# A fused attention and deformable-convolution block: the front's steps in halves, the convolution's PSUM emptied by ScalarE

## The chip, the cores and the metric

The kernel runs on one core of a Trainium2 chip. The metric is device time in microseconds (us) of one execution, lower is better. The engines are TensorE (PE; its weight loads are listed apart as PEld), VectorE (DVE), ScalarE (ACT), GpSimd (POOL) and the queue of SyncE (SP), which only issues transfers. Each engine works through its own list of instructions in the order in which the kernel wrote it.

## The reference

Two layers, each with a residual, on x of shape 8 x 256 x 64 x 64 in float32. `_gn` is a group normalisation over 32 groups.

```
x = x + L0(_gn(x))     # L0: q, k, v by a 1x1 convolution; 4 heads; softmax over the 3x3
                       # neighbours of each pixel; a second set of 3x3 weights generated from
                       # q, k, v; alpha * generated + beta * softmax weights v; projection
x = x + L1(_gn(x))     # L1: modulated deformable 3x3 convolution: a 3x3 convolution gives
                       # offsets and masks; each of 9 taps samples 4 corners of the image at
                       # its offset, mixes them bilinearly, times the mask; then 256x9 -> 256
```

## The kernel before, in words

One image is held in SBUF (`image`), in 8 chunks of 8 rows (512 pixels). Its work falls in two parts. The *front* is layer 0 and the preparation of layer 1: `attention(b)` runs the normalisation and the attention chunk by chunk, and `prepare(b)` writes the second normalisation's result to a table in DRAM (`to_table`), computes the offsets (`offsets`) and turns them into indices and weights (`positions`). The *back* is the deformable convolution. A chunk has 9 taps; a tap of a chunk is a *slot*, so an image has 72 slots, and a slot has 4 blocks of 128 pixels.

For each block of the back POOL gathers 128 table entries of 4 KB (`gather`), ACT scales the first corner (`scale`), DVE adds the three others (`sum_corners`, three instructions per block), PE turns the sum (`transposes`, two per block into `pt`), ACT copies `pt` to SBUF (`vt`), and PE multiplies by the tap's weights (`product`, four matmuls into the PSUM tile `po`, which gathers all 9 taps of a chunk in two banks, one for each half `m` of the output channels). After the ninth tap `finished` adds x1, the result of layer 0, to `po` and stores it. x1 was written to DRAM by `second_stats` (`kept`) and is read back into `r` in the middle of the chunk.

The loop at the end of `preact_kernel` (L891 to L910) writes out the order by hand for PE, ACT, DVE and POOL. It merges the back of image b with the front of image b+1. Slot n is: `transposes(n)`; `ahead(4n)`, which scales blocks 8 and 9 ahead, sums blocks 6 and 7 ahead (six DVE instructions) and gathers blocks 18 and 19 ahead; `product(n-1)`; then the front's steps that are due; then `ahead(4n+2)`. After every ninth tap both `ahead`s stand before `product`, and `finished` after it. The front is a generator that yields 73 times per image; the pace lets about one step run in each slot. A chunk of attention is seven steps, named below by what they hold: *q* (L579 to L583: `spread_weights` of the chunk before, then q), *k*, *products*, *logits*, *v0*, *v1*, *weights* (the last with `project(1)`, the add into x1, the statistics and `keys(0)`). The first image's front runs alone, before any slot; the last image's back runs alone, after all fronts.

Lines that matter below: `psum_a` (L190) hands out four PSUM buffers in turn for all of the front. `spread_weights` (L487) fills all four with `wk` matmuls (L492), and DVE empties them by multiplying with a mask (L500). `q` (L288) then asks for the same buffers (L293). `finished` (L856) has DVE read `po` (L859). `po` has a single buffer, so the next chunk's first tap (L848) waits until it has been read.

Of the kernel before, what the change touches and what calls it, by code (L numbers as in the profile page):

```python
# [17 lines left out]
P = 128  # L18
C = 256
# [33 lines left out]
STEPS = 2 + 7 * NC + 6 + NC + 1  # L53
STEPS_AHEAD = 6
# [3 lines left out]
def preact_kernel(ctx: ExitStack, tc: tile.TileContext, a: dict, out: bass.AP):  # L58
# [126 lines left out]
    wp = ctx.enter_context(tc.tile_pool(name="wp", bufs=NC + 3))  # L185
# [93 lines left out]
    class Attention:  # L279
# [70 lines left out]
        def products(self):  # L350


            self.qk = qk = p1.tile([P, NB, NT, 2, NK], F32, tag="qk", name=f"qk_{self.u}")
            for jj in range(NB // 2):
                both = [psum_a(f"qk_{self.u}_{jj}_{h}") for h in range(2)]
                for ct in range(NT):
                    for j in range(2):
                        for t in range(2):
                            o = 2 * (2 * jj + j) + t
                            for h in range(2):  # L360
                                r = slice(64 * h, 64 * h + 64)
                                n = (2 * j + ct) * NK
                                nc.tensor.matmul(  # L363
                                    both[h][64 * t : 64 * t + 64, n : n + NK],
                                    self.qt[r, ct, o * T * T : (o + 1) * T * T],
                                    kt[r, ct, :, T * o : T * o + KT],
                                    start=True,
                                    stop=True,
                                )
                for h in range(2):  # L370
                    nc.vector.tensor_mul(  # L371
                        qk[:, 2 * jj : 2 * jj + 2, :, h, :],
                        both[h][:, : 4 * NK].rearrange("p (j c k) -> p j c k", j=2, c=NT),
                        near_k.unsqueeze(1).unsqueeze(1).to_broadcast([P, 2, NT, NK]),
                    )

        def logits(self):
# [3 lines left out]
            by = p1.tile([P, G * KT, 3], F32, tag="by", name=f"by_{self.u}")  # L381
# [94 lines left out]
        def weights(self):  # L476
            ps = psum_a(f"w_{self.u}")
            for j in range(NB):
                nc.tensor.transpose(
                    ps[:, j * P : (j + 1) * P],  # L480
                    wts2[self.c % 2][:, j].rearrange("p h k -> p (h k)"),
                    ident,
                )
            self.wsb = p1.tile([P, N], F32, tag="wsb", name=f"wsb_{self.u}")
            nc.scalar.copy(self.wsb, ps)
# [38 lines left out]
        def weighted(self, i):  # L524
            n = N // NH
            if i == 0:
                self.acc = p1.tile([P, NT, N], F32, tag="acc", name=f"acc_{self.u}")
# [30 lines left out]
        def second_stats(self):  # L558
            for ct in range(NT):
# [3 lines left out]
                )  # L563
            s = slice(self.c * N, (self.c + 1) * N)
            nc.sync.dma_start(kept[self.b % 2][:, :, s], self.xt[:, :, s])

    def attention(b):
# [6 lines left out]
        gn = gn.ready()  # L574
        xn = normed(xt, gn, 0)
        yield None
        d = None
        for c in range(NC):
            a_ = Attention(b, c, xn, stats)  # L579
            if d:  # L580
                d.spread_weights()
            a_.q(0)
            a_.q(1)  # L583
            yield None
            a_.k(0)
            a_.k(1)
            yield None
            a_.products()
# [4 lines left out]
            if d:  # L593
                d.keys(1)
                d.carry_v()
            a_.generated()
# [3 lines left out]
            a_.v(0)  # L600
            if d:
                d.weighted(1)
            a_.turned()
            a_.softmax_2()
            if c + 1 < NC:
                xn = normed(xt, gn, c + 1)
            yield None
            a_.v(1)
            if d:
                d.add(0, d.project(0))  # L610
            a_.softmax_3()
            yield None
# [3 lines left out]
            a_.weights()  # L616
# [5 lines left out]
        d.weighted(0)  # L622
        d.keys(1)
# [3 lines left out]
        for m in range(NT):  # L627
            d.add(m, d.project(m))
        d.second_stats()
        gn = Norm(stats, f"1_{b}")  # L630
        yield None
        gn.means()
        yield None
        yield gn.ready()

    def prepare(b, gn):
# [5 lines left out]
        def to_table(c, xn):  # L642
            for i in range(TJ // 2):
# [9 lines left out]
                ts = p2.tile([TP, 2, C], F32, tag="ts", name=f"ts_{b}_{c}_{i}", bufs=4)  # L653
# [89 lines left out]
        xn = normed(xt, gn, 0)  # L743
        om = None
        for c in range(NC):
            if om is not None:
                positions(c - 1, om)
            to_table(c, xn)
            om = offsets(c, xn)
# [13 lines left out]
        yield  # L763

    found: dict = {}

    def fronts():
        for b in range(B):
            gn = None
            for got in attention(b):  # L770
                gn = got
                if gn is None:
                    yield
            yield
# [62 lines left out]
    def product(b, n):  # L837
        c, k = divmod(n, KK)
        if k == KK // 2:
            r = p1.tile([P, NT, N], F32, tag="r", name=f"r_{b}_{c}")  # L840
            nc.sync.dma_start(r, kept[b % 2][:, :, c * N : (c + 1) * N])
            state["r"] = r
        if k == 0:
            state["po"] = ps_o.tile([P, NT, 512], F32, tag="o", name=f"po_{b}_{c}")
        po, v = state["po"], state.pop(("v", n))
        for m in range(NT):
            for ct in range(NT):
                nc.tensor.matmul(  # L848
                    po[:, m, :],
                    w_conv[:, ct, k, m * P : (m + 1) * P],  # L850
                    v[:, ct, :],
                    start=(k == 0 and ct == 0),
                    stop=(k == KK - 1 and ct == NT - 1),
                )

    def finished(b, c):  # L856
        po, r = state["po"], state["r"]
        for m in range(NT):
            nc.vector.tensor_add(r[:, m], po[:, m], r[:, m])  # L859
# [10 lines left out]
    with tc.manual_schedule(engines=ordered):  # L870
# [20 lines left out]
        for n in range(B * SLOTS + 1):  # L891
# [3 lines left out]
            if n < B * SLOTS:  # L895
                transposes(*divmod(n, SLOTS))
                ahead(NB * n)
                if last:
                    ahead(NB * n + 2)
            if n > 0:  # L900
                product(*divmod(n - 1, SLOTS))
            if last:
                finished(*last)

# [84 lines left out]
```

## Time and profile before

| | |
|---|---|
| median of 3 runs | 5517.69 us (5511.05 to 5520.15) |
| the profiled execution's own time | 5149.96 us |
| its span on the core | 5148.2 us |
| mean granted TensorE clock in it | 0.962 |
| PE busy / DVE busy / ACT busy / POOL busy | 4726.1 / 4206.1 / 2374.4 / 3193.9 us |
| DMA | 1422.61 MB, mean 276 GB/s |
| first image's front alone, up to the first `pt` transpose | 0 to about 351.6 us |
| last image's back alone | about 4689.6 to 5148.2 us |

The profiled execution was 6.7% shorter than the median. Durations in the profile are of that execution. A matmul of float32 stands in the trace as two records, and records overlap: 512 columns take about 0.43 us from start to start, though one record reads 0.59 us. The groups list for each line the busy time, the mean of one, and the idle time of the engine just before, with what ended it.

### The profile page before, as it was taken

The numbers are of one execution on the slowest core, as the hardware profiler recorded it, in microseconds if no ns is written. First come the engines' busy times: TensorE is split into PE (matmuls) and PEld (weight loads), VectorE is DVE, ScalarE is ACT, GpSimd is POOL, SyncE is SP. The second block draws the span as 40 slices with busy tenths as digits, with TensorE's granted clock in tenths as the row PEclk, the third lists the DMA queues.
The fourth block names the chain that finished last, engine by engine and source line by source line (L and its number), as shares of the span: only waits on it lengthen the run. The fifth ranks groups of instructions, "written<-read, shape, count | busy, mean of one in ns | idle before, by whom it ended". The sixth has DMA issues, their size and how long they took to land. (4 is left out here: it accounts for less than half of the span.)

```text
span 5148.2 us, 79694 instructions
## 1 busy us (share of the span) xinstructions
PE 4726.1 (92%) x26592; PEld 2641.3 (51%) x26592; DVE 4206.1 (82%) x10128; ACT 2374.4 (46%) x5184; POOL 3193.9 (62%) x2310
## 2 busy tenths in 40 slices
PE   6979998999999999999999999999999999999888
PEld 4545554555545555455554555555554555554444
DVE  4568787878888888888888888888888888888888
ACT  2334444444444444454444444444444444444544
POOL 0027675666666666676665766756666566666776
PEclk9989999999999999999999999999999999999999
DMA  2067777887788777977779777888778877788998
GB/s 92 17 217 264 250 277 283 289 278 265 270 315 294 272 263 272 331 284 265 266 267 345 277 269 269 289 309 281 262 269 310 309 265 269 261 306 316 391 375 348
DMA packets 476841, 1422.61 MB, mean 276 GB/s; under 512 B 46910, under 2 KB 114750, under 8 KB 476300
## 3 DMA queue, kind: packets, MB, share of 16 engines
q0 software_dynamic: 331776, 1208.11, 66.1%
q1 hardware_dynamic: 141902, 204.27, 11.0%
q10 hardware_dynamic: 2750, 5.12, 0.3%
q8 instruction: 210, 3.44, 0.3%
q14 instruction: 203, 1.66, 0.1%
HBM read 1280.19 MB, written 137.13 MB: 275 GB/s over the span
## 5 line engine op out<-in xcount | busy, mean ns | idle before, releaser
L786 POOL DMA_INDIRECT g<-table,idx x2304 | 3191.4, 1385 | 1933.4 <-DVE s L810 513.4
L810 DVE SCALAR_TENSOR_TENSOR s<-g,wt,s 128x256 f32<-128x256 f32 x6912 | 2797.5, 476 | 401.3 <-ACT s L802 390.5
L848 PE MATMUL po<-vt,w_conv 128*128 128x512 f32 x4608 | 2142.0, 609 | 72.5 <-DVE r L859 72.5
L848 PEld LDWEIGHTS po<-vt,w_conv 128*128 128x128 f32 x4608 | 856.6, 196 | 947.0 <-issue 866.7
L802 ACT ACTIVATE s<-g,wt 128x256 f32<-128x256 f32 x2304 | 1081.8, 509 | 545.3 <-DMA g<-table,idx 473.3
L831 PE MATMUL pt<-ident,s 128*128 128x128 f32 x4608 | 693.5, 284 | 104.9 <-DVE s L810 73.0
L831 PEld LDWEIGHTS pt<-ident,s 128*128 128x128 f32 x4608 | 519.5, 143 | 401.9 <-DVE s L810 121.3
L834 ACT COPY vt<-pt 128x512 f32<-128x512 f32 x1152 | 611.5, 583 | 162.5 <-PE pt L831 161.7
L293 PE MATMUL psq<-xn,w_qkvT 128*128 128x512 f32 x512 | 288.0, 713 | 113.3 <-DVE wk L500 111.6
L301 ACT COPY q<-psq 128x512 f32<-128x512 f32 x128 | 75.0, 586 | 484.0 <-PE psq L293 484.0
L668 PE MATMUL om<-xn,w_off 128*32 128x512 f32 x2304 | 292.7, 605 | 0.0
L325 PE MATMUL psv<-xn,w_qkvT 128*128 128x264 f32 (+1 forms) x1088 | 263.9, 388 | 0.0
L293 PEld LDWEIGHTS psq<-xn,w_qkvT 128*128 128x128 f32 x512 | 111.4, 228 | 287.8 <-DVE wk L500 167.5
L371 DVE TENSOR_TENSOR qk<-qk,near_k 128x400 f32<-128x400 f32 x256 | 128.9, 565 | 158.6 <-PE qk L363 158.6
L325 PE MATMUL psk<-xn,w_qkvT 128*128 128x264 f32 (+1 forms) x1088 | 246.6, 381 | 2.1 <-ACT k L338 2.1
L325 PEld LDWEIGHTS psv<-xn,w_qkvT 128*128 128x128 f32 x1088 | 202.9, 193 | 84.5 <-issue 49.9
L545 PE MATMUL proj<-acc,w_projT 128*128 128x512 f32 x512 | 238.1, 592 | 0.7 <-ACT acc L540 0.7
L325 PEld LDWEIGHTS psk<-xn,w_qkvT 128*128 128x128 f32 x1088 | 202.2, 190 | 62.3 <-issue 18.9
L347 ACT COPY v<-psv 128x320 f32<-128x320 f32 (+1 forms) x272 | 110.1, 418 | 238.1 <-PE psv L325 238.0
L540 ACT COPY acc<-av 128x512 f32<-128x512 f32 x128 | 74.9, 585 | 265.1 <-PE av L533 264.7
L338 ACT COPY k<-psk 128x264 f32<-128x264 f32 (+1 forms) x272 | 100.6, 372 | 204.2 <-PE psk L325 204.0
L500 DVE TENSOR_TENSOR wk<-wk,near 100x512 f32<-100x512 f32 x256 | 158.5, 680 | 34.6 <-PE wk L492 34.6
(91 smaller groups left out, 3342.0 us busy)
## 6 DMA issues: line engine op xcount, KB each, us to landing
table<-ts SPq DMA_DIRECT2D x384, 176.0 KB
g<-table,idx POOLq DMA_INDIRECT x2304, 6.7
x<-in_x_dram SPq DMA_DIRECT2D x64, 512.0 KB
x<-x SPq DMA_DIRECT2D x64, 512.0 KB
r<-x SPq DMA_DIRECT2D x64, 512.0 KB
out_dram<-r SPq DMA_DIRECT2D x64, 512.0 KB
w_conv<-in_w_conv_dram ACTq DMA_DIRECT2D x1, 2304.0 KB
w_qkv<-in_w_qkv_dram ACTq DMA_DIRECT2D x2, 384.0 KB
```

Of the source, the lines that this page charges most:

```text
L293: nc.tensor.matmul(ps, w_qkvT[:, ct, m * P : (m + 1) * P], window(self.xn, ct, 4), start=(ct == 0), stop=(ct == NT - 1),)
L325: nc.tensor.matmul(ps[:, : (hi - lo) * WP], w_qkvT[:, ct, o : o + P], self.xn[:, ct, lo:hi, :], start=(ct == 0), stop=(ct == NT - 1),)
L371: nc.vector.tensor_mul(qk[:, 2 * jj : 2 * jj + 2, :, h, :], both[h][:, : 4 * NK].rearrange("p (j c k) -> p j c k", j=2, c=NT), near_k.unsq ...
L500: nc.vector.tensor_mul(wk.rearrange("p (t n) -> p t n", n=T * T), ps[:NK].rearrange("p (t n) -> p t n", n=T * T), near.unsqueeze(1).to_bro ...
L545: nc.tensor.matmul(ps, w_projT[:, ct, m * P : (m + 1) * P], self.acc[:, ct].rearrange("p (t y x) -> p y t x", y=T, x=T), start=(ct == 0), ...
L668: nc.tensor.matmul(ps[32 * g : 32 * g + 32, :], w_off[:, ct, k, :], window(xn, ct, k), start=(n < 4), stop=(n >= KK * NT - 4),)
L786: nc.gpsimd.indirect_dma_start(out=g, out_offset=None, in_=tables[b % 2], in_offset=bass.IndirectOffsetOnAxis(ap=found[b, c][0][:, j, k : ...
L802: nc.scalar.activation(s, g[:, 0:C], AF.Copy, scale=w[:, 0:1])
L810: nc.vector.scalar_tensor_tensor(s, g[:, q * C : (q + 1) * C], w[:, q : q + 1], s, ALU.mult, ALU.add)
L831: nc.tensor.transpose(pt[ct][:, j, :], s[:, ct * P : (ct + 1) * P], ident)
L834: nc.scalar.copy(v[:, ct, :], pt[ct].rearrange("p b n -> p (b n)"))
L848: nc.tensor.matmul(po[:, m, :], w_conv[:, ct, k, m * P : (m + 1) * P], v[:, ct, :], start=(k == 0 and ct == 0), stop=(k == KK - 1 and ct = ...
```

## The change

- Every step of the front is cut in about two: 144 steps per image instead of 73, and the pace counts in half slots. `products` takes one of its two halves at a time. `spread_weights` and `q` are now different steps; so are `project(0)` with its add and `project(1)`; `to_table` and `offsets`; and the first normalisation has a step of its own.
- A slot is now: `transposes(n)`, `ahead(4n)`, the matmuls of `product` for m = 0, a half step; then `ahead(4n+2)`, the matmuls for m = 1, a half step.
- Inside a chunk `softmax_3` comes before the first projection's add, `normed` for the next chunk after it, and `weights` before `project(1)`.
- After the ninth tap ACT copies each half of `po` to a new SBUF tile `y` right behind that half's matmuls; at the end of the slot DVE adds x1 to `y` for both halves in one instruction (`stored`).
- The last image's x1 is neither written to DRAM nor read back: `stored` takes it from `image`.
- The row buffers `ts` for the table go from 4 to 6. To make room, `by`, `wsb` and `acc` share the buffers of `tw`, `gs` and `q`, and the pool of indices and weights goes from 11 to 10.

```diff
-STEPS = 2 + 7 * NC + 6 + NC + 1
-STEPS_AHEAD = 6
+STEPS = 2 * SLOTS
+STEPS_AHEAD = 12
...
+            if self.b + 1 == B:
+                return
             s = slice(self.c * N, (self.c + 1) * N)
             nc.sync.dma_start(kept[self.b % 2][:, :, s], self.xt[:, :, s])
...
             if d:
                 d.spread_weights()
+            yield None
             a_.q(0)
             a_.q(1)
             yield None
             a_.k(0)
+            yield None
             a_.k(1)
             yield None
-            a_.products()
+            a_.products(0)
+            yield None
+            a_.products(1)
             if d:
                 d.weighted(0)
             yield None
             a_.logits()
             if d:
                 d.keys(1)
                 d.carry_v()
+            yield None
             a_.generated()
             a_.softmax_1()
             a_.carry_k()
             yield None
             a_.v(0)
+            yield None
             if d:
                 d.weighted(1)
             a_.turned()
             a_.softmax_2()
+            yield None
+            a_.v(1)
+            a_.softmax_3()
+            yield None
+            if d:
+                d.add(0, d.project(0))
             if c + 1 < NC:
                 xn = normed(xt, gn, c + 1)
             yield None
-            a_.v(1)
-            if d:
-                d.add(0, d.project(0))
-            a_.softmax_3()
-            yield None
+            a_.weights()
             if d:
                 d.add(1, d.project(1))
                 d.second_stats()
-            a_.weights()
+            yield None
             a_.keys(0)
             yield None
...
+    def finished(b, c, m):
+        if m == 0:
+            state["y"] = p1.tile([P, NT, N], F32, tag="y", name=f"y_{b}_{c}")
+        nc.scalar.copy(state["y"][:, m], state["po"][:, m])
+
+    def stored(b, c):
+        r, y = state["r"], state["y"]
+        x1 = r if b + 1 < B else image[:, :, c * N : (c + 1) * N]
+        nc.vector.tensor_add(r, y, x1)
         nc.sync.dma_start(
             out[b].rearrange("(t p) l -> p t l", p=P)[:, :, c * N : (c + 1) * N], r
         )
...
-            if n < B * SLOTS:
-                transposes(*divmod(n, SLOTS))
-                ahead(NB * n)
+            for m in range(NT):
+                if n < B * SLOTS:
+                    if m == 0:
+                        transposes(*divmod(n, SLOTS))
+                    ahead(NB * n + 2 * m)
+                if n > 0:
+                    product(*divmod(n - 1, SLOTS), m)
                 if last:
-                    ahead(NB * n + 2)
-            if n > 0:
-                product(*divmod(n - 1, SLOTS))
+                    finished(*last, m)
+
+                h = NT * n + m + 1
+                goal = h * STEPS + min(h, STEPS) * STEPS_AHEAD
+                while (done - STEPS) * STEPS < goal:
+                    next(steps, None)
+                    done += 1
             if last:
-                finished(*last)
-
-            goal = (n + 1) * STEPS + min(n + 1, SLOTS) * STEPS_AHEAD
-            while (done - STEPS) * SLOTS < goal:
-                next(steps, None)
-                done += 1
-            if n < B * SLOTS and not last:
-                ahead(NB * n + 2)
+                stored(*last)
```

## The prediction

> **What bounds the kernel now.** First the page's head: PE is busy for 92% of the span, DVE for 82%.
>
> ```profile
> span 5148.2 us, 79694 instructions
> ...
> PE 4726.1 (92%) x26592; PEld 2641.3 (51%) x26592; DVE 4206.1 (82%) x10128; ACT 2374.4 (46%) x5184; POOL 3193.9 (62%) x2310
> ```
>
> Shares over the whole span mix three stages, so next the busy times by stretch, cut where an image's first `pt` transpose starts. Columns: stretch, its length, busy time of PE, PEld, DVE, ACT, POOL, clock, DMA share, GB/s.
>
> ```profile
> 2862.70:3483.80 621.10, 581.58 (x3321) 327.78 (x3320) 524.44 (x1267) 294.93 (x649) 411.07 (x288) 0.97 0.81 285
> 4689.60:5148.20 458.60, 398.29 (x1242) 189.49 (x1240) 388.21 (x941) 219.78 (x455) 344.62 (x298) 0.92 0.93 364
> ```
>
> An image beside the next one's front takes 621 us; PE is idle for 39.5 of them, and a clock of 0.97 loses some 20 more. DVE is at 84%. The last image alone is another case: its DMA share is 0.93 at 364 GB/s. There PE hardly counts.
>
> Now one chunk of attention, slot by slot (the same columns; in order q, k, products, logits, v0, v1, weights), and below it a q slot in which a chunk of the convolution ends.
>
> ```profile
> 1877.00:1888.88 11.88, 9.47 (x34) 4.01 (x33) 11.88 (x27) 4.08 (x9) 10.36 (x6) 1.00 0.76 249
> 1888.88:1896.75 7.87, 7.87 (x33) 5.39 (x32) 5.42 (x14) 4.29 (x10) 6.35 (x6) 1.00 0.82 264
> 1896.75:1903.85 7.10, 7.10 (x113) 4.66 (x112) 4.18 (x10) 2.95 (x7) 5.25 (x6) 1.00 0.98 366
> 1903.85:1911.03 7.18, 7.18 (x33) 3.56 (x29) 7.11 (x16) 4.58 (x10) 3.78 (x2) 1.00 0.60 225
> 1911.03:1918.71 7.68, 7.68 (x61) 5.12 (x60) 6.20 (x16) 4.87 (x12) 4.98 (x4) 1.00 0.78 262
> 1918.71:1926.57 7.86, 7.86 (x30) 4.69 (x29) 6.95 (x18) 4.61 (x11) 5.37 (x4) 1.00 0.81 268
> 1926.57:1933.91 7.34, 7.34 (x34) 4.42 (x32) 7.00 (x16) 3.56 (x8) 3.78 (x5) 1.00 0.79 265
> 1695.25:1713.47 18.22, 12.24 (x34) 5.10 (x33) 16.01 (x36) 5.10 (x11) 15.93 (x8) 0.81 0.74 236
> ```
>
> PE fills six of seven slots to the last 10 ns. Only q has a hole, 2.4 us here and 6.0 us with a clock of 0.81 in the last row. DVE's timeline in the first q slot says why.
>
> ```profile
> 1878.66 1.27 DVE L560 BATCH_NORM_STATS2 stats<-x 128x6 f32<-128x512 f32 x2
> 1879.86 4.82 DVE L810 SCALAR_TENSOR_TENSOR s<-g,wt,s 128x256 f32<-128x256 f32 x12
> 1884.60 2.47 DVE L500 TENSOR_TENSOR wk<-wk,near 100x512 f32<-100x512 f32 x4
> ```
>
> PE ends the `wk` matmuls at about 1883.1, but DVE has 12 corner sums of two `ahead`s queued in front of the multiply that frees q's PSUM buffer. In the longer slot 18 sums and both adds of `finished` stand there. The waits of PE over five images (995.83 to 4109.6; total, times, longest) order the holes:
>
> ```profile
> PE psq L293 <- DVE wk L500: 80.8, 35, 5.8
> PE pt L831 <- DVE s L810: 33.3, 69, 1.6
> PE po L848 <- DVE r L859: 25.6, 16, 3.1
> PE pt L831 <- ACT vt L834: 16.2, 9, 3.1
> PE ptab L648 <- DVE xn L242: 12.9, 10, 2.7
> PE gt L415 <- ACT v L347: 12.4, 5, 4.0
> ```
>
> These are 181 of 200 us of idle PE, 40 per image.
>
> **What the Trainium skill says.** "TensorE: Matmul & The Clock Gate", Part 1, calls VectorE and ScalarE strict FIFOs and lets PE pull only weight loads ahead; the q slot agrees, since nothing passes the sums on DVE or the blocked q on PE. The same part says that an idle window of about 3.4 us halves PE's clock until it has been busy again. The trace fits: the slot with 2.2 us of waiting has a clock of 1.00, the one with 5.8 us has 0.81. The summary table of "PSUM — Partial Sum Buffer" wants a read beside running matmuls to be in another bank. ACT's copy of half 0 of `po` beside the matmuls of half 1 is in another bank; no run here shows such a read, since L859 reads `po` only when both halves are done.
>
> **The change part by part**, against the profiled 5150 us.
>
> *Halves.* I add up the fourteen halves of a chunk, PE against DVE. Spacings are from the timelines: transposes of a slot 0.87, half a product 4 x 0.43 = 1.72, q 3.45, half of k or v 1.78, half of the `qk` 0.87, `weighted` 1.07, half of `keys` 0.87, gen 1.75, `turned` 0.3, a projection 1.72, `weights` 0.44, `wk` 1.0. DVE: six sums 2.4; half of the `qk` masks 0.97; `logits` 3.1; `softmax_1` 0.6; `turned` with `softmax_2` 1.1; `softmax_3` 2.8; an add 0.6; `normed` 1.3; statistics 1.2; four `wk` 2.4. PE sums to 53.3, DVE to 49.3. DVE's lag behind PE at the end of each half is the lag before, plus DVE's work, minus PE's, and not below what the half's own PE results allow: products 0 ends 1.0 behind; products 1, 0; logits 2.8; gen 1.5; v0 0.4; turned 1.1; v1 2.8; add 0, 2.8; add 1, 3.1; keys 2.0; spread 4.1. In the spread half the first `wk` multiply ends 1.8 before DVE's end, so 2.3 us after PE has left. PE now has transposes and half a product, 2.59 us, before q asks for that buffer. So the hole closes, with 0.3 us to spare. From 80.8 us I leave 20, for chunk ends and late gathers.
>
> *ACT empties `po`.* Two copies of 128x512 from PSUM, 0.58 us each by L834's row, replace two DVE adds (1.28 together); the first runs behind matmuls of the other half, and the second has at least 0.87 us of transposes and a half step before the next `po` matmul. L859's 25.6 go. ACT, 46% busy, takes 64 x 1.17 = 75 us, on no path while PE leads; behind a copy that waits for PE stand two scales, whose sums come one `ahead` later. DVE's single add of 128x1024 in SBUF is not in the trace; L430 (144 elements, 308 ns) and L457 (432, 607) give 1.04 ns per element and 160 fixed, so 1.2 us, from 0.9 (two instructions of 640 elements of L242 took 1.1 us) to 1.36 (two adds as before). I take 1.2, within 0.1 of the old pair, and behind the steps.
>
> *Other holes.* `ptab` waiting for `normed` (12.9): the separate step puts 2.59 us of PE between; gone. `gt` behind `v` (12.4) comes from slots with two whole steps; halves space these; gone. Half of the `vt` waits and all of the 7.8 for `qk` masks (in the same answer) go; the 33.3 for sums stay, since as much DVE work precedes them as before. Of `gn`'s 7.4 nothing is counted. Idle time falls from 200 to about 70 per five images (200 - 61 - 26 - 13 - 12 - 8 - 8), 26 us per image.
>
> *Clock.* It loses about 20 us per image; with the long holes gone I take back 12, bounds 0 and 20.
>
> *Sum of the steady part.* It runs from 351.6 to 4689.6, which is 6.97 images of 622 us: 6.97 x (26 + 12) = 265 us.
>
> *First front alone.* In each chunk PE waits 2.0 us for `wts` (L479 behind L467), since the add of the first projection delays `softmax_3`. Now `softmax_3` stands first. Seven or eight times 1.5: 10 us.
>
> *Last image.* Its eight reads of x1 (4.2 MB) leave a stage at 364 GB/s: 11.5 us if DMA alone limits, 0 if not; I take 10. The eight writes saved earlier lie where the DMA share is 0.80: nothing.
>
> *At nothing.* `ts` with six buffers removes ACT waits of 49 us, but PE is full in those slots (11.01 us each); without that cover, 49 at most. `by`, `wsb` and `acc` take buffers whose last readers stand earlier on the same engine or before the matmuls that feed the new writer. Ten index buffers serve eight new chunks and the two in use. GpSimd's order is the same, and SyncE's lacks the sixteen transfers; the table's writes come half a slot earlier.
>
> Total 265 + 10 + 10 = 285: 5150 becomes 4865, a ratio of 0.945. The medians are 7.1% above the profiled execution for a reason that the profile doesn't show. If it scales both kernels alike, 5517.7 x 0.945 = 5212.
>
> **Rivals.**
>
> *The slower runs are slower on PE.* If PE's clock is lower there throughout, DVE catches up and the holes are already closed. For 368 us more with no steady idle left, PE would need 368 + 280 us on some 4050 busy, 16%. Then only the two 10s and a few tens of microseconds remain: about 5470. A part of it gives 5300 to 5400. For it: PE is what the clock touches. Against: three runs agree within 0.2%, and nothing in the trace shows it.
>
> *The clock recovers more.* If the extra 368 us are half-clock windows set off by the holes, these go too: about 4950 to 5050. For it: the 0.81 above. Against: the profiled run lost only 3.8%.
>
> *Slower: DVE becomes the bound.* Place: the spread half, where DVE is 4.1 us behind and the margin is 0.3. Every microsecond by which DVE is later there (scales late on ACT, because the exponential of `logits` waits for DVE on the same queue) is one on PE, 56 times. The 285 us are used up at 5.1 us more per chunk, a lag of over 9; from there the kernel is slower, and at 7 it would be 4865 + 392 = 5257 profiled, 5630 on the medians' scale. For it: DVE at 84% would be at 524/583, 90%. Against: scales stand one `ahead` before their sums, and four halves out of fourteen are light on DVE.
>
> *No change:* the halves close the q hole and open others of the same size: 5515.
>
> **How the numbers follow.** Likeliest (5130 to 5300, from idle recovered of 20 to 35 and clock of 5 to 18 per image): 0.60. Slower PE, in full or in part (5300 to 5480): 0.21. More clock (under 5130): 0.10. No change 0.03, slower 0.06. The range for 8 in 10 takes the likeliest, most of the faster case and the lower half of the slow-PE case: 5030 to 5420. About 0.2% is what a measurement can tell from nothing; the cases give faster 0.91, same 0.03, slower 0.06.
>
> **What would show it.** After, q's wait for `wk` should be under 25 us per five images and L859's wait gone; PE idle per image near 14 us and the image near 583 us; clock about 0.98 there; the last image's stage about 448 us. A new wait of PE on DVE in the transposes or q, with DVE full through spread and keys, would speak for the slower rival. A profile as predicted with a median near 5470 would speak for the slower PE. The likeliest way to be wrong is the step from the profiled scale to the medians.

## The result and the profile after

The kernel after takes 5530.19 us (median of 20 executions, 5512.14 to 5556.52). The kernel before takes 5518.56 us beside it (20 executions, 5499.78 to 5537.86). The ratio is 1.0016, with a 95% interval of 1.0003 to 1.0029. The forecast was 5212 us and a ratio of 0.945; its range of 5030 to 5420 did not hold the time.

One thing must be said first, because no number below can be read without it. The execution whose profile stood ahead of the prediction (5149.96 us) was of another kind than the timed runs of the same kernel (5511 to 5520 us). In the experiments every visit to a chip showed one kind throughout; the *first* kind below is that of the listed profile, the *second* that of the timed runs. The profile after is of the second kind, so it can't be set against the profile before line by line; `after_3` further down is the same kernel on a chip of the first kind.

The head of the page of the kernel after:

```profile
span 5537.7 us, 79485 instructions
...
PE 4910.2 (89%) x26592; PEld 2745.7 (50%) x26592; DVE 4187.2 (76%) x10064; ACT 2456.7 (44%) x5312; POOL 3015.0 (54%) x2310
```

The span is 390 us longer than the profiled span of before, and PE is busy for a smaller share of it (89% against 92%). Next the busy times by stretch of the kernel after: an image beside a front, the last image alone, and two slots of one chunk (q with half of k, and two slots later the second half of the products with `weighted` and `logits`). The columns are those of the prediction: stretch, length, busy time of PE, PEld, DVE, ACT, POOL, clock, DMA share, GB/s.

```profile
2354.62:3016.11 661.49, 606.82 (x3322) 341.54 (x3321) 521.86 (x1259) 306.02 (x665) 377.63 (x288) 0.94 0.76 268
4948.10:5537.70 589.60, 419.70 (x1257) 209.37 (x1255) 388.06 (x940) 227.30 (x478) 408.74 (x298) 0.85 0.73 276
2438.43:2451.00 12.57, 11.68 (x36) 5.94 (x33) 12.57 (x29) 4.23 (x9) 9.68 (x5) 0.86 0.83 286
2458.05:2475.46 17.41, 12.89 (x93) 7.90 (x90) 9.88 (x21) 3.61 (x8) 8.80 (x10) 0.71 0.82 300
```

The loss has a place: the last row. One slot takes 17.41 us, with PE idle for 4.5 of them and the clock at 0.71 in it. The mean of this slot over the 56 chunks whose front runs beside a back, worked out from the starts of the `pt` transposes, is 15.85 us. The waits of PE over five images of the kernel after (1026.21 to 4343.70; total, times, longest) name it:

```profile
PE qk L364 <- issue: 138.2, 201, 2.2
PE av L534 <- issue: 34.3, 56, 1.6
...
PE psq L293 <- DVE wk L501: 11.3, 21, 0.8
PE po L870 <- ACT y L881: 10.9, 8, 2.5
```

The hole at q is closed (80.8 us before, 11.3 now). In its place PE stands still in the small `qk` and `av` matmuls, and "issue" says that it waited for nothing that the profile shows. PE's timeline in the 17.41 us slot, from the first `qk` of its half on:

```profile
2460.79 1.18 PE L364 MATMUL qk<-k,q 64*64 64x100 f32 x21
2463.03 0.40 PE L364 MATMUL qk<-k,q 64*64 64x100 f32 x3 [1.05 <-issue]
...
2468.77 1.99 PE L534 MATMUL av<-wk,vk 100*64 100x64 f32 x32 [0.83 <-issue]
```

GpSimd's timeline of the same moments:

```profile
2457.18 0.94 POOL L805 DMA_INDIRECT g<-table,idx  x1 [0.30 <-issue]
...
2464.94 0.94 POOL L805 DMA_INDIRECT g<-table,idx  x1 [0.32 <-DVE s L829]
2466.18 0.94 POOL L805 DMA_INDIRECT g<-table,idx  x1 [0.30 <-issue]
```

From 2454.5 to 2467.1 ten gathers go out one behind the other, most of them 1.25 us apart (a *burst*). PE, which did 21 `qk` matmuls without a stop, then does the rest one, two or three at a time; it begins `av` 1.7 us after the burst has ended. An obvious suspect is the fetch of PE's own instructions, but the DMA records speak against it: no packet of a queue of the kind `instruction` starts between 2451.0 and 2470.5 us, while PE stops and starts again seven times. PE's signals are late as well. In the waits of the whole kernel, the view writes "remote" where an engine was released later than anything on record explains:

```profile
DVE qk L372 <- remote: 406.7, 66, 11.3
...
ACT vt L853 <- remote: 339.1, 62, 10.4
```

Both wait for PE alone: VectorE's mask behind the `qk` matmuls, ScalarE's copy behind the transposes. The profile of before that the prediction read has no such line.

### The profile page after: what moved, and what is told of

Read it like the earlier page. It is cut to its first block, busy times and chain, and to the rows that moved or that the text cites. A ratio compares the mean times of both kernels' runs of the same rounds, so it can differ in the third digit from the quotient of the medians.

```text
span 5537.7 us, 79485 instructions
## 1 busy us (share of the span) xinstructions
PE 4910.2 (89%) x26592; PEld 2745.7 (50%) x26592; DVE 4187.2 (76%) x10064; ACT 2456.7 (44%) x5312; POOL 3015.0 (54%) x2310
## 2 busy tenths in 40 slices
DMA packets 472486, 1414.18 MB, mean 255 GB/s; under 512 B 46654, under 2 KB 114494, under 8 KB 471948
## 3 DMA queue, kind: packets, MB, share of 16 engines
q14 instruction: 201, 1.65, 0.1%
## 5 line engine op out<-in xcount | busy, mean ns | idle before, releaser
L805 POOL DMA_INDIRECT g<-table,idx x2304 | 3012.5, 1308 | 2498.6 <-DVE s L829 963.1
L870 PE MATMUL po<-vt,w_conv 128*128 128x512 f32 x4608 | 2315.0, 630 | 96.8 <-ACT y L881 58.2
L850 PE MATMUL pt<-ident,s 128*128 128x128 f32 x4608 | 673.3, 288 | 152.9 <-ACT vt L853 95.4
L850 PEld LDWEIGHTS pt<-ident,s 128*128 128x128 f32 x4608 | 551.2, 147 | 398.5 <-issue 208.2
L364 PE MATMUL qk<-k,q 64*64 64x100 f32 x4096 | 219.7, 268 | 200.0 <-issue 186.1
L364 PEld LDWEIGHTS qk<-k,q 64*64 64x64 f32 x4096 | 142.8, 139 | 331.4 <-issue 291.8
L293 PE MATMUL psq<-xn,w_qkvT 128*128 128x512 f32 x512 | 237.9, 606 | 21.2 <-DVE wk L501 19.2
L534 PE MATMUL av<-wk,vk 100*64 100x64 f32 x4096 | 204.6, 257 | 49.2 <-issue 46.8
L534 PEld LDWEIGHTS av<-wk,vk 100*64 100x64 f32 x4096 | 174.2, 166 | 128.5 <-issue 104.0
L521 ACT COPY vk<-vk 100x512 f32<-100x512 f32 x256 | 138.1, 590 | 140.7 <-PE vk L516 138.1
```

The source lines that it names most:

```text
L293: nc.tensor.matmul(ps, w_qkvT[:, ct, m * P : (m + 1) * P], window(self.xn, ct, 4), start=(ct == 0), stop=(ct == NT - 1),)
L364: nc.tensor.matmul(both[h][64 * t : 64 * t + 64, n : n + NK], self.qt[r, ct, o * T * T : (o + 1) * T * T], kt[r, ct, :, T * o : T * o + KT ...
L534: nc.tensor.matmul(av[64 * h : 64 * h + 64, g, t * T * T : (t + 1) * T * T], self.vk[:, t, o : o + 64], self.wk[2 * g + h][:, i * n + t * ...
L805: nc.gpsimd.indirect_dma_start(out=g, out_offset=None, in_=tables[b % 2], in_offset=bass.IndirectOffsetOnAxis(ap=found[b, c][0][:, j, k : ...
L850: nc.tensor.transpose(pt[ct][:, j, :], s[:, ct * P : (ct + 1) * P], ident)
L870: nc.tensor.matmul(po[:, m, :], w_conv[:, ct, k, m * P : (m + 1) * P], v[:, ct, :], start=(k == 0 and ct == 0), stop=(k == KK - 1 and ct = ...
```

## The experiments

Two theories went into the first runs. *Burst theory*: gathers that GpSimd issues back to back hold up PE's small matmuls and its signals, and the new order puts long bursts at the products. *Split theory*: the halves of the products cost their time by themselves, through PSUM buffers and masks. In a later form the first is called theory H: whether bursts hold PE up depends on the chip.

**Was the listed profile usual?** The kernel before, unchanged, was profiled again.

> The kernel before, unchanged, looked at again, because its 20 timed executions have a median of 5518.56 us and its one profile a span of 5148.2. Theory A (the profiled execution was an outlier, and PE usually runs out of instructions in the small qk matmuls of the products step, as in the profile after): a span near 5518, PE idle put down to issue ahead of qk of 100 us or more, a last image's back of 550 us or more where the old profile has 459. Theory B (the profile is representative, and only the repeated executions are slower, by a lower clock): a span near 5150, no PE idle ahead of qk put down to issue.

It took 5476.26 us (a single execution) with a span of 5474.5, so the listed profile was not usual. PE's waits in it, over the whole span:

```profile
PE pt L831 <- ACT vt L834: 130.7, 33, 10.1
PE psq L293 <- DVE wk L500: 107.8, 44, 5.8
PE qk L363 <- issue: 71.1, 152, 1.2
```

The "issue" waits are here before the change too, at 71.1 us; after it they are 186.1 in the same view. In this trace the `qk` matmuls of a chunk take about 2.5 us from the first start to the last where a row of two gathers lies over their start, and 5.5 to 8.8 where a row of 10 to 14 gathers ends 3.1 to 6.8 us into them. In the listed profile they take 1.4 to 1.6, whatever gathers lie over them. The trace of e0_before has "remote" lines too, the largest with 165.0 us for `vt`.

**Pacing, bytes, whole products, q one step later.** Four kernels on one chip. In a_paced, the kernel after, a memset of 128x512 stands behind each gather (and `ts` has 5 buffers, to make room):

```diff
...
+    idle = p1.tile([P, 512], F32, tag="idle", name="idle")
...
             in_offset=bass.IndirectOffsetOnAxis(ap=found[b, c][0][:, j, k : k + 1], axis=1),
         )
+        nc.gpsimd.memset(idle, 0.0)
```

In a_rows_1k, the kernel after, each gather fetches 1 KB of a 4 KB entry, and the sums read that first corner three times:

```diff
-            out=g,
+            out=g[:, 0:C],
...
-                    s, g[:, q * C : (q + 1) * C], w[:, q : q + 1], s, ALU.mult, ALU.add
+                    s, g[:, 0:C], w[:, q : q + 1], s, ALU.mult, ALU.add
```

In a_whole_products, the kernel after:

```diff
             a_.products(0)
-            yield None
             a_.products(1)
+            yield None
             if d:
                 d.weighted(0)
```

And in b_split_q, the kernel before, q leaves the step of `spread_weights` and joins that of k, so that this step now holds both:

```diff
                 d.spread_weights()
+            yield None
             a_.q(0)
             a_.q(1)
-            yield None
             a_.k(0)
```

> The kernel after, with a memset of 128x512 on GpSimd behind every gather (and one table row buffer fewer, to make room). Nothing else changes; the pitch of gathers issued back to back goes from 1.25 us to about 1.75 us. Burst theory (while GpSimd issues gathers back to back PE's small matmuls and its signals are held up, and the new order puts bursts of 10 to 13 gathers at the products): the step of products falls from 9.6-12.7 us towards 3, the slot with products(1) from 15.8 to under 12, an image from 664 to 630-645, the time to 5330-5450. Split theory (the halves of products themselves cost it, by PSUM buffers and masks on DVE): no change, 5500-5560, or slower by what late gathers add. If the memset disturbs DVE more than the bursts disturb PE, the corner sums on DVE are longer than 478 ns and the time rises.

> The kernel after, but each gather fetches only the first 1 KB of its 4 KB table entry, and the three corner sums read that same first corner: a quarter of the bytes with as many gather instructions and the same arithmetic on every engine. If it is the bytes in flight that hold PE up: the products step falls to about 1.5 us, the last image's back from 590 to 450 or less, the time to 5150-5300. If it is the issue of the gathers by GpSimd: the products step stays at 9 us or more wherever a burst of 10 covers it, images beside a front stay at 650-665, and only the last image's back may shorten; 5380-5520. Split theory: as the second.

> The kernel after, with both halves of products in one half step and weighted(0) alone in the next, as many steps as before. Split theory: the 6 us by which the slot with products(1) is longer than its like in the kernel before come back at least in a third, 2 us x 64, and the time is 5400 or less. Burst theory: the products still stand behind three half steps in which DVE has little but corner sums and so under a burst of gathers; 5490-5560, products step 9 us or more.

> The kernel before, with q moved one step later, in front of k, so that a slot stands between the wk matmuls and q; nothing else. If closing the hole at q is worth what it measures: PE's wait for wk falls from 108 us per five images to under 30, images shorten by 12 us or more, time 5420-5450. Burst theory: the time saved at q comes back ahead of the products, one slot later, since DVE's sums and so the gathers run on through the same slots; products slots grow by 1 us or more, time 5480-5530.

On this chip the kernel before took 5141.39 us, about the time of the listed profile. No run on it has a "remote" line, so nothing could be told here about bursts; all four expectations had been made for the other kind. Measured: paced 5107.48, ratio 0.9928 (0.9909 to 0.9946); 1 KB rows 4828.38, ratio 0.9385 (0.9367 to 0.9403); whole products 4888.32, ratio 0.9515 (0.9489 to 0.9540); q one step later 5182.96, ratio 1.0072 (1.0052 to 1.0092).

The last of these is a result of its own, and a miss: a gain had been expected if the wait at q was worth what it measures, and here the kernel got 42 us slower. PE's waits of b_split_q over the whole span:

```profile
PE pt L831 <- DVE s L810: 104.3, 184, 10.5
PE po L848 <- DVE r L859: 97.0, 43, 4.2
PE av L533 <- DVE qk L371: 47.9, 14, 6.0
PE psk L325 <- ACT q L301: 45.1, 9, 6.3
```

The 111.6 us at q are gone from this view, but `pt` waits 31 us more than in the listed profile and `po` 24 more, `av` waits 48 where it waited 9, and `psk`, the matmuls of k, waits 45 for ScalarE's copy of q where it didn't wait for it. The last of these comes with q and k in one step: k asks for PSUM buffers that q has just filled. For the others, as I read it, VectorE's backlog had been waited off at q, and without that wait it is waited off at the next places; no run isolates this, and none gives q a step of its own.

**The kernel after on each kind of chip.** Then the kernel after itself, paced and with 1 KB rows, on one chip.

> The kernel after, unchanged, beside the kernel before on one chip. Theory H (the chip decides: on one kind, where the kernel before takes about 5145 us, PE's signals are never late; on the other, 5480 to 5520 us, they are late under bursts of gathers): where the kernel before takes 5130-5160 the kernel after takes 4860-4900, a ratio of 0.945-0.955; where it takes 5470-5530 the ratio is 0.995-1.005. Rival (the halves of products cost their own time everywhere, and the version with whole products is faster for that): 5000-5100 where the kernel before takes 5145.

> The kernel after with a memset behind every gather, again, beside the kernel after. Where the kernel before takes about 5145 us: 5090-5120, as before, which is what the memsets cost by themselves. Where it takes 5480-5520: by theory H with the issue of the gathers as the cause, the products step falls under 4 us and the time to 5100-5300, below the kernel after on the same chip although the memsets cost 200 us where nothing is held up; if pacing doesn't matter, 5650-5800.

> The kernel after with gathers of 1 KB per entry and sums that read the same first corner three times, again. Where the kernel before takes about 5145 us: 4820-4835. Where it takes 5480-5520: if the bytes in flight hold PE up, 4830-4950, nearly as on the other chip; if it is the number of gathers issued back to back, 5300-5500, with products steps of 9 us or more under bursts of 10.

Here the kernel before took 5516.63 us (39 executions), the kernel after 5529.50 (ratio 1.0026, 1.0011 to 1.0042), paced 5125.11 (ratio 0.9283, 0.9264 to 0.9301), and 1 KB rows 5517.06 (0.9993, 0.9977 to 1.0008). So the time that the change loses comes back when GpSimd pauses between gathers, and not when each gather fetches a quarter of the bytes (5300 to 5500 had been expected for that). The traffic of a_rows_1k_2, and its waits:

```profile
DMA packets 251302, 508.22 MB, mean 92 GB/s; under 512 B 46654, under 2 KB 114494, under 8 KB 250764
```

```profile
ACT vt L853 <- remote: 499.5, 72, 13.6
DVE qk L372 <- remote: 418.8, 66, 11.5
...
PE qk L364 <- issue: 220.8, 300, 1.8
```

A third of the traffic (508 MB against 1414) and about half of the packets (251302 against 472486) leave late signals and stops as they were. In a_paced_2 they are all but gone (7.3 us of "remote" waits, none at `qk`); the groups on POOL show what the pause is:

```profile
L806 POOL DMA_INDIRECT g<-table,idx x2304 | 2865.2, 1244 | 980.9 <-DVE pos L719 388.4 <-DVE s L831 206.3 <-issue 199.5
L812 POOL MEMSET idle<- 128x512 f32 x2304 | 1259.2, 547 | 1.1
```

The memsets add 1259 us of work to GpSimd and the kernel gets 404 us faster. Gathers in a row now start 1.65 us apart instead of 1.25. From the start of the first to that of the last `qk` matmul of a chunk (half a `product` between them) it takes 4.4 us in a_paced_2, as where nothing is held up (4.4 in after_3), against 10.2 in after_2. The mean clock is 0.970, the same as in a_paced on the other chip, against 0.933 in after_2: with the stops gone, nothing is left of the lower clock.

**Confirmation on the first kind, the kernel before paced, a shorter pause.** In b_paced the memset of 128x512 stands behind each gather of the kernel before (`wsb` takes the buffers of `gs`, to make room); in a_paced_256 the memset of a_paced is half as long:

```diff
-    idle = p1.tile([P, 512], F32, tag="idle", name="idle")
+    idle = p1.tile([P, 256], F32, tag="idle", name="idle")
```

> The kernel after, unchanged, for the chip on which the next three run. Theory H: where the kernel before takes 5130-5160 us, 4860-4900 (ratio 0.945-0.955, the forecast's own ratio); where it takes 5470-5530, a ratio of 0.995-1.005.

> The kernel before with a memset of 128x512 on GpSimd behind every gather (and wsb in the buffers of gs, to make room). If bursts of gathers hold up the kernel before too where it takes 5480-5520 us: it falls to 5150-5400 there, image beside a front under 640. If the kernel before is slow there for another reason (clock, DMA): no change or slower, 5480-5700. Where it takes about 5145: the memsets cost 50-220 us, 5190-5370.

> The kernel after with a memset of 128x256 behind every gather (about 0.3 us instead of 0.54; one table row buffer fewer). If any gap between gathers is enough: 4880-5000 on either kind of chip, below the 5107-5125 of the longer memset, since GpSimd then keeps up better with DVE. If the gap has to be of some length: where the kernel before takes 5480-5520, 5150-5450 with products steps of 4 us or more under bursts.

> The kernel after with both halves of products in one half step and weighted(0) alone in the next, again. Where the kernel before takes about 5145 us: 4880-4910, as measured, and no better than the kernel after. Where it takes 5480-5520: the products still stand behind half steps with little but corner sums on DVE, so 5490-5560; if the division of products is what puts them under the burst, 5400 or less.

The kernel before took 5149.32 us on this chip, and the kernel after 4900.97: a ratio of 0.9524 (0.9507 to 0.9541). The forecast's ratio was 0.945, and its time on the profiled scale 4865. Paced before: 5339.18. Pause of 128x256: 4966.89 (0.9654). Whole products: 4890.43 (0.9505, 0.9489 to 0.9521), 10 us under the kernel after, with intervals that overlap: the division of the products costs next to nothing here, and the split theory falls for this kind of chip. Busy times by stretch in after_3, an image, the last image, and the same two slots of a chunk as above:

```profile
2100.03:2683.18 583.15, 569.31 (x3321) 321.54 (x3320) 521.09 (x1258) 307.81 (x665) 378.75 (x289) 0.99 0.84 304
4387.33:4898.10 510.77, 403.99 (x1257) 199.44 (x1255) 389.14 (x940) 231.12 (x478) 375.99 (x298) 0.88 0.83 319
2177.86:2187.45 9.59, 9.59 (x36) 5.43 (x33) 9.59 (x22) 4.23 (x9) 8.68 (x4) 1.00 0.84 296
2194.49:2201.87 7.38, 7.38 (x93) 4.93 (x90) 7.05 (x17) 3.83 (x8) 5.55 (x7) 1.00 0.97 351
```

The same slot that took 17.41 us takes 7.38. Over the 56 chunks its mean is 7.45 us against 15.85 in the profile after, which makes 470 of the 629 us between the two kinds of chip. There is a burst here too (twelve gathers, most of them 1.25 us apart, from 2190.9 to 2206.3), and PE's timeline runs through beneath them:

```profile
2193.63 0.93 PE L364 MATMUL qk<-k,q 64*64 64x100 f32 x32
...
2197.23 0.93 PE L364 MATMUL qk<-k,q 64*64 64x100 f32 x32
2198.09 1.15 PE L534 MATMUL av<-wk,vk 100*64 100x64 f32 x32
```

**The same pauses on the second kind of chip, and the last image.** What remained was the kernel before paced, the shorter pause where signals are late, and the last image's back, which is 511 us in after_3 against 462.5 before.

In a_stored_later, the kernel after, the add of x1 stands behind the sums of the next slot's first half:

```diff
+        due = None
...
                     ahead(NB * n + 2 * m)
+                if due and m == 0:
+                    stored(*due)
...
-            if last:
+            if last and n == B * SLOTS:
                 stored(*last)
+            due = last
```

In a_dve_empties, the kernel after, VectorE adds x1 from PSUM right behind each half (`finished`), there is no `y`, and `stored` only sends `r`:

```diff
...
-        nc.scalar.copy(state["y"][:, m], state["po"][:, m])
...
+        nc.vector.tensor_add(r[:, m], state["po"][:, m], x1[:, m])
...
```

> The kernel after with a memset of 128x256 behind every gather, again. Where the kernel before takes about 5145 us: 4955-4985 as measured. Where it takes 5480-5520: if a gap of some 0.6 us between gathers (0.33 of memset and the issue of it) is enough, 4960-5010, as on the other chip; if it needs the longer memset, 5150-5450.

> The kernel before with a memset of 128x512 behind every gather, again. Where the kernel before takes about 5145 us: 5320-5345. Where it takes 5480-5520: if its 370 us above the other chip are gathers issued back to back as well, 5330-5370, so that with the memsets the change is worth the same ratio (5125/5345 = 0.959) on both; if they have another cause, 5500-5700.

> The kernel after with the add of x1 (stored) moved half a slot later, behind the sums of the next slot's first half, so that VectorE doesn't stand still for ScalarE's copy y at the end of a chunk. If that wait is what makes a second slot of 11 us in each chunk of the last image (VectorE then runs 30 sums without a pause, and a gather issued beneath them takes 9.97 us): the last image's back falls by 20-48 us; where the kernel before takes about 5145, 4850-4880 against 4901; where it takes 5480-5520, 5450-5520, still held up at the products. If the long gather comes from somewhere else: within 8 us of the kernel after.

The kernel before took 5485.92 us on this chip. The shorter pause gave 5277.70 (0.9617, 0.9573 to 0.9661): 311 us more than on the other kind of chip, so a memset of 0.33 us (gathers 1.43 us apart) takes back part and one of 0.55 (1.65 us apart) nearly all (5125 against 5107). The kernel before paced gave 5417.85 (0.9883, 0.9853 to 0.9912), where 5330 to 5370 had been expected: it falls by 68 us although its memsets cost 190 on the other chip. So bursts slow the kernel before too, and most but not all of its excess goes with them: 79 us are left against the other chip, where 337 were. Its `qk` matmuls still take 2.0 us against 1.4 there; what else is left isn't known. The later add gave 5475.13 (0.9994), no gain here.

> The kernel after with the add of x1 half a slot later, again. Where the kernel before takes about 5145 us: if VectorE's wait for the copy y makes the second slot of 11 us in each chunk of the last image, its back is 463-490 us instead of 511 and the time 4850-4880; if not, 4890-4915. Where it takes 5480-5520: within 0.3% of the kernel before, as measured.

> The kernel after with VectorE emptying po again: for each half one add of x1 straight from PSUM, right behind the half's matmuls; no y. Where the kernel before takes about 5145 us: if ScalarE's copies were what the last image's back lost by, it is 463-490 us instead of 511; beside a front PE waits for po again (25 us per five images), so that 4870-4910 follows; if the second long slot stays, it comes from the new order of the slot (sums, half a product, sums), not from the copies. Where it takes 5480-5520: 5500-5560.

> The kernel after with both halves of products in one half step and weighted(0) alone in the next. Where the kernel before takes about 5145 us: 4885-4895. Where it takes 5480-5520: if the products are held up by the burst wherever they stand near it, 5450-5560; if the division of products has a part, under 5400.

This last chip was the one of after_3 again, and again of the first kind (before 5146.17): the later add 4871.82 (0.9457, 0.9429 to 0.9485), VectorE emptying `po` 4889.14 (0.9505) and whole products 4890.54. Hence whole products were never run on a chip that holds PE up, and whether they would lose less there stays open. For the last image the answer is clear. Its back as one stretch, first in a_stored_later_2, then in a_dve_empties:

```profile
4395.63:4867.93 472.30, 395.69 (x1257) 195.65 (x1255) 390.01 (x940) 230.69 (x478) 351.06 (x298) 0.92 0.89 345
```

```profile
4415.43:4878.94 463.51, 391.19 (x1257) 194.27 (x1255) 389.50 (x949) 221.84 (x460) 339.77 (x298) 0.92 0.90 351
```

The two edits take back 38 and 47 us of the 48. Beside a front, though, a_dve_empties loses: over five images PE waits 56.9 us there for VectorE to read `po`, where it waits 28.3 for ScalarE in after_3, and the whole kernel is only 12 us under after_3. So ScalarE's copies pay beside a front and cost in the last image. VectorE and GpSimd in after_3, at the end of one chunk of the last image, show what stands behind the loss there:

```profile
4553.60 1.23 DVE L886 TENSOR_TENSOR r<-y,x 128x1024 f32<-128x1024 f32 x1 [2.86 <-ACT y L881]
4554.74 11.96 DVE L829 SCALAR_TENSOR_TENSOR s<-g,wt,s 128x256 f32<-128x256 f32 x30
4571.11 0.48 DVE L829 SCALAR_TENSOR_TENSOR s<-g,wt,s 128x256 f32<-128x256 f32 x1 [4.41 <-ACT s L821]
```

```profile
4557.55 9.97 POOL L805 DMA_INDIRECT g<-table,idx  x1 [3.06 <-DVE s L829]
```

VectorE waits 2.86 us for ScalarE's copy `y`, then has 30 sums to catch up with and does them without a gap. A gather issued beneath them isn't done until 0.8 us after the last. Nine such gathers of 10 us stand in the last image's back, about one to a chunk, and with them go slots of 11 to 12 us four slots behind each chunk's end. That VectorE's wait for the copy is the cause is shown by the edits, after which these slots are gone from nearly every chunk; the part of the long gather in it is read off the trace.

## Why the prediction was wrong

*The step that failed* is "If it scales both kernels alike, 5517.7 x 0.945 = 5212" (with the ratio unrounded). The prediction named this step as its likeliest way to be wrong, but gave no case in which the extra time depends on the order of the gathers. The medians' extra time was no scale factor on the profiled execution. Most of it is PE being held up under back-to-back gathers, of which the listed profile shows nothing, and its size depends on the order of the work. From one kind of chip to the other the kernel before goes from 5149 to 5517 us (367 more), the kernel after from 4901 to 5530 (629 more). The change gains 248 us of its own and pays 262 more than the kernel before on a chip of the second kind; that the two cancel is chance. An image beside a front shows the payment in after against after_3: 661.49 against 583.15 us, of which 40.8 are more idle time of PE (54.67 against 13.84) and 37.5 more busy time, at a clock of 0.94 instead of 0.99.

Why the new order pays more was read off the traces and not isolated by a run: in the half steps q, k(0) and k(1) VectorE now has little but corner sums, so buffers come free and GpSimd issues nine gathers or more in a row just where the products' small matmuls stand. Counting as a row gathers that start less than 1.7 us apart, a row of nine or more lies over the `qk` matmuls in 55 of 56 chunks of the kernel after, and in 28 of 56 in e0_before. In e0_before the `qk` matmuls of these 28 take 5.3 us from the first start to the last end, and of the 26 with rows of at most three 2.7. That the rows cause the stop is shown, by the pauses; all of them are memsets, and no run spaces the gathers by other means. How a gather holds up PE isn't shown. The prediction had counted "four halves out of fourteen are light on DVE" as a safeguard; it did not ask what a VectorE with nothing else to do would set free.

*The steps on the profiled scale* are to be judged on after_3.

- The q hole: 20 us left of 80.8 was forecast; 2.5 are left in after_3, and 11.3 where bursts hold PE up. Right. In after_3 the same 12 sums stand ahead of the same multiply on VectorE as in the prediction's first q slot:

```profile
2174.27 4.82 DVE L829 SCALAR_TENSOR_TENSOR s<-g,wt,s 128x256 f32<-128x256 f32 x12
2179.01 2.47 DVE L501 TENSOR_TENSOR wk<-wk,near 100x512 f32<-100x512 f32 x4
```

  PE comes to q at 2180.51 and doesn't wait. b_split_q closed the hole too, and lost: closing it is not yet a gain, and what the halves elsewhere add to it no run isolates.
- "L859's 25.6 go": wrong as a sum, though with VectorE reading `po` in the new order (a_dve_empties) the wait would be 56.9. Its place is taken by PE's wait for ScalarE's `y`, here over five images of after_3 (932.79 to 3850.74), with what else stands there:

```profile
PE po L870 <- ACT y L881: 28.3, 15, 5.3
PE gv L216 <- DVE gnd L211: 16.4, 7, 3.1
PE qk L364 <- ACT k L338: 12.3, 5, 2.8
...
PE psq L293 <- DVE wk L501: 2.5, 10, 0.3
PE pt L850 <- DVE s L829: 2.3, 5, 0.5
```

- "The 33.3 for sums stay": they fell to 2.3. `gt` and `vt` are gone from the list, and `ptab` is at 6.0 in the same answer. These gains and the misses (`po`, and `gv` and `qk` behind k's copy, which weren't foreseen) cancel: idle per image was forecast near 14 us and is 13.84 in the image above, so that the total is met partly by luck.
- Clock: 0.98 forecast, 0.99 measured. Image: 583 forecast, 583.15 measured. The steady part, cut at the same slot in both, gains 280 us where 265 was forecast.
- The first front alone: 10 us forecast; the first `pt` transpose comes at 333.3 instead of 351.6, 18 us. The wait that was named, for `wts`, falls from 17.2 to 4.9 us there; where the other 6 come from isn't known.
- The last image: 10 us of gain forecast, 48 us of loss measured (510.77 against 462.5, both from the 499th slot on; the prediction's row began 4 us later). The step that put ScalarE's copies "on no path while PE leads" (PE doesn't lead there) and the one that left the add of x1 at its place without asking what VectorE waits for there failed together. What leaving out the transfers of x1 is worth alone wasn't measured. The DMA share fell from 0.93 to 0.83, so transfers didn't limit.
- VectorE's single add of 128x1024: 1.2 us forecast, 1.23 measured.

The sum on that scale was 285 us and is 250 (from 5148.2 to 4898.1): the working of the steady part held. Of the rivals, "the slower runs are slower on PE" asked about the right 368 us, but took PE's clock for their cause; they are stops, and the clock of 0.94 comes with them (a_paced_2, without the stops, has 0.970 on a chip of the second kind). "No change: the halves open others of the same size" was given 0.03, and is what the 20 executions show, though on a chip of the first kind no holes of that size open. DVE as the bound did not appear.

## What to carry to other kernels

When the profiled execution is several per cent off the timed ones, the missing time may be a wait in one place, as here, and not a scale; find out where it lies, or put the whole forecast in doubt, before carrying a gain over. A kernel that issues indirect gathers back to back beside dense small matmuls may be held up on some chips: a pause of 0.55 us on GpSimd behind each gather made this one 7.2% faster than the kernel before on one chip and 0.7% on another, one of 0.33 us 3.8% and 3.5%, and without a pause it was 0.3% slower and 4.8% faster. And an engine emptied of work doesn't just wait: as the traces read here, VectorE ran ahead, and what it set free, the gathers, went out all at once.

## What the runs showed of the hardware

- The same program takes two times, by chip as far as these runs go. The experiments went to five chips: the kernel before took 5141.39 and 5149.32 (5146.17 at another visit) on two, and 5485.22, 5485.92 and 5516.63 on three. Why chips differ isn't known from these runs.
- On the second kind, gathers issued every 1.25 us hold up PE's small matmuls and its signals to other engines; another engine waits for up to 11.3 us in the kernel after. A quarter of the gathered bytes per entry changes next to nothing (5517.06 against 5529.50), a pause of 0.55 us in GpSimd's queue removes nearly all of it (5125.11 against 5107.48 where nothing is held up), 0.33 us removes a part (5277.70 against 4966.89).
- An indirect gather issued beneath an unbroken run of corner sums ended 0.8 us after the run: 9.97 us instead of 0.94. The Trainium skill, "SBUF — State Buffer", section "SBUF: two separate sides", calls the pair of ports that VectorE and GpSimd share an exclusive lock, which a VectorE instruction with two SBUF inputs takes against a GpSimd instruction that reads SBUF; the sums have two SBUF inputs. The same section tells of a `tensor_tensor` that didn't stall a DMA from GpSimd's queue. That these gathers, which take their indices from a tile in SBUF, are held up by the sums fits the lock, but no run isolates it; and others of 0.94 us run under six sums (2462.16 in the kernel after), so that it isn't every sum that holds one up.
